# Where the second steps of a cross attention may place their divisions and layer-norm portions on VectorE

## The chip, the cores and the metric

The kernel runs on one core of one Trainium2 chip. The metric is the device time of one execution in microseconds (us). A core has a matrix engine (TensorE, PE in the profile, with its weight loads as PEld), a vector engine (VectorE, DVE), an activation engine (ScalarE, ACT), a general engine (GpSimd, POOL) and a queue that issues transfers (SyncE, SP). Each engine works through its own list of instructions in order, and waits on semaphores for the others.

## The reference, cut to what matters

The reference is one decoder layer in float32 over x of 16 batch elements, 112 tokens each, 512 features: self attention, cross attention over a context of 375 rows for each batch element, and a feed-forward part.

```python
q, k, v = heads(hs @ Wq.T + bq), heads(at @ Wk.T + bk), heads(at @ Wv.T + bv)   # 16 heads of 32
scores = clip(q k^T / sqrt(32), -50, 50); masked keys get -50
probs = softmax(scores)
ctx = probs @ v
delta = residual_scale * (ctx @ Wo.T + bo)
x = x + layernorm(delta) * ln_gamma + ln_beta
x = x + FFN(layernorm(x))        # after the cross attention
```

The change touches only the order of the cross attention's work. What is computed stays the same.

## The kernel before, in words

The kernel is written in a framework that traces instructions in the order of the program and then plans an issue order for each engine. TensorE is the exception: its order is that of the program. For the other engines the planner runs the program against a clock of its own, and whenever an engine is free it takes, of the instructions that are ready by that clock, the one that was traced first. So an instruction that was traced late can be issued early, if its inputs are there and the engine is free. `tc.issue_after(ins)` limits that: what the block traces on the engine of `ins` is queued behind `ins` in that engine's list. It adds no wait for another engine.

The cross attention runs over 16 batch elements b, and in each over three chunks kc of 125 keys. This text calls one turn of `cross.step` (line 1318) step (b, kc), and (b, 1) the second step of its batch element. A step lays, in this order:

- TensorE's 32 score matmuls of its keys (`scores`, line 929);
- ScalarE's two exponentials of them (line 1330), into tiles es for kc = 0 and e for the others;
- for the step before, called `late` in the code: TensorE's weighted values (`weigh`, line 940); VectorE's two additions of its e to es (`add`, line 1367), only if that step had kc = 1 or 2; and, if it had kc = 2, TensorE's key sums (line 951), ScalarE's copies of sums and values (lines 1376 and 1378), and a new generator `self.parts` with the divisions;
- ScalarE's check of the scores (line 1338);
- filler work for TensorE (`f.fill`), a queue of pieces that is worked off by estimated microseconds;
- portions of `self.parts`: two of them if kc = 1, the rest if kc = 2. A portion (`quotients`, line 1381) is a reciprocal (line 1383) and a multiplication (line 1384) on VectorE. Where b is a multiple of 4, all four are laid in the first step, with no tie.

The main loop then lays portions of `finish`, again only where kc > 0 and b is no multiple of 4: three portions for b = 1, 5, 9, 13, two for b = 2, 6, ..., three for b = 3, 7, .... In block 1 `finish` holds the second layer norm's rest (a reciprocal root of some 12 small instructions, lines 784 to 796, then one normalised row tile for each portion, line 802). In blocks 5 and 9 it holds the cross attention's own layer norm: a reciprocal root (with line 1287), then one row tile for each portion (lines 1291, 1299, 776 and 777), then the third layer norm's root and normalised tiles. It is used up in blocks 1, 6 and 10.

Both kinds of portions are laid under `issue_after(self.last)`, and `self.last` is the latest addition of line 1367. In step (b, 2) that is the addition of the step's own turn, for (b, 1). In step (b, 1) no addition is laid, so `self.last` is still that of step (b, 0), which belongs to the third chunk of batch element b - 1.

The filler of a block makes the keys and values of the next batch element. The first values are one product of eight matmuls (line 902), which VectorE copies out of its bank (line 907). The others come from seven block products for the values (line 1073, taken out by VectorE at lines 1076 and 1078) and seven for the keys (line 1013, taken out at lines 1035, 1023 and 1019), laid in turns; they are called r1 to r7 and k1 to k7 below. In odd blocks four products for queries follow (line 884, taken out by ScalarE at line 892). All these products, and the key sums, take turns in three PSUM banks with the tag mm: TensorE cannot begin a product before the bank of an earlier one has been emptied. VectorE also makes the sums of the context's blocks (line 979), and GpSimd one copy of keys (line 1203).

```python
            if b > 0 and kc > 0:
                with tc.issue_after(self.last):
                    for _ in range(2 if kc == 1 else C):
                        next(self.parts, None)
...
            if bl > 0 and kc > 0:
                with tc.issue_after(cross.last):
                    for _ in range(2 + bl % 2):
                        next(finish, None)
```

Of the kernel before, what the change touches and what calls it, by code (L numbers as in the profile page):

```python
# [597 lines left out]
def finite_layer(  # L598
# [30 lines left out]
    nc = tc.nc  # L629
# [22 lines left out]
    def pair(name, tag="e", bufs=3):  # L652
        return evp.tile([P, 2, HG, S], F32, tag=tag, name=name, bufs=bufs)
# [267 lines left out]
    def scores(k_of, q_of, rows_):  # L921

        scs = [psum("sc", [P, 2, 512]) for _ in range(2)]
        views = [
            s[:rows_, :, : HG * S].rearrange("p i (j s) -> p i j s", j=HG) for s in scs
        ]
        for j in range(C):
            for i in range(HG):
                nc.tensor.matmul(  # L929
                    views[i // 2][:, i % 2, j, :], k_of(i, j), q_of(i, j), start=True, stop=True  # L930
                )
        return views
# [179 lines left out]
    class SelfAttention:  # L1112
# [35 lines left out]
        def step(self, b, grp, f, us, prepared):  # L1148
            b, v, es = self.next
            if b + 1 < B:  # L1150
                self.begin(b + 1, grp)
            with tc.issue_after(self.behind.ins):
                for _ in range(prepared):
                    next(w2_prep, None)
            first = max(0.45 * us, min(us, 5.5))
            f.fill(first)
            eTs = []
            for e, share in zip(es, (0.45 * (us - first), 0.35 * (us - first))):
                tr = psum("sc", [P, 2, 512])
                trv = tr[:S, :, : HG * S].rearrange("p i (j s) -> p i j s", j=HG)  # L1160
                for i in range(2):
                    for j in range(C):
                        nc.tensor.transpose(trv[:, i, j, :], e[:, i, j, :], ident[:S, :S])  # L1163
                eT = pair("eT")
                nc.scalar.copy(eT[:S], trv)
                eTs.append(eT)
                f.fill(share)
            y = psum("ys", [P, C, S])
            weighted_values(y, v[b % GB][:S], eTs, True, True)
            nc.scalar.copy(xyT[:, :, ts(b, S)], y)  # L1170
            f.drain()
# [96 lines left out]
    class AfterCross:  # L1268
# [15 lines left out]
        def finish(self):  # L1284
# [23 lines left out]
                yield 0.0  # L1308
            yield from self.norm.steps()

    class Cross:


# [4 lines left out]
        def step(self, b, kc, q, keys, f, us):  # L1318
            scs = scores(
                lambda i, j: keys.third(keys.k[ds(i * DH, DH), j], kc),  # L1320
                lambda i, j: q[ds(i * DH, DH), j, ts(b % 2, S)],
                KP,
            )
            n = b * KC + kc
            late = self.late

            es = [(pair("es", "es", 3) if kc == 0 else pair("e"))[:KP] for _ in scs]
            self.late = (b, kc, keys.v[kc][:KP], es)
            for i, sc in enumerate(scs):
                nc.scalar.activation(  # L1330
                    es[i], sc, AF.Exp, scale=scl[:, n : n + 1], bias=bia[:, n : n + 1]
                )
            self.weigh(late)
            for i in range(2):
                self.add(late, i)
            self.divide(late)
            for i, sc in enumerate(scs):
                nc.scalar.activation(  # L1338
                    sc,
                    sc,  # L1340
                    AF.Relu,
                    scale=nscl[:, n : n + 1],
                    bias=limit[:KP, :1],
                    accum_out=low[:KP, 2 * n + i : 2 * n + i + 1],
                )
            if kc == 0 and b % GB == 0:
                for _ in self.parts:
                    pass
            f.fill(us)
# [4 lines that stand above are left out]
# [504 lines left out]
    def at_once(pieces):  # L1858
        run(pieces)
        yield from ()  # L1860

    def tiles_of(pieces):

        for _ in pieces:
            next(pieces, None)
            yield

    def tiles_of(pieces):
# [5 lines left out]
    late = itertools.chain(  # L1874
        itertools.repeat(None, 1),
        n3[2].transposes(),
        tiles_of(after[1].projections()),
        at_once(after[1].finish()),
        itertools.repeat(None, 3),
        n3[3].transposes(),  # L1880
    )
# [40 lines left out]
@with_exitstack  # L1922
def decoder_layer(ctx: ExitStack, tc: tile.TileContext, *args):
    nc = tc.nc
    flag = ctx.enter_context(tc.tile_pool(name="flag", bufs=1))
    unfit = flag.tile([1, 1], I32, name="unfit")
    finite_layer(tc, unfit, *args)
    with tc.If(nc.values_load(unfit, min_val=0, max_val=1, skip_runtime_bounds_check_because="a comparison gives 0 or 1") > 0):
        general_layer(tc, *args)
# [49 lines left out]
```

## Time and profile before

| what | value |
|---|---|
| median of 3 runs | 1358.8 us (1357.83 to 1360.26) |
| the profiled execution | 1359.02 us |
| its span, first to last instruction | 1357.2 us |
| TensorE busy | 1335.8 us of the span |
| VectorE busy | 819.8 us of the span |
| granted TensorE clock, mean | 0.998 |
| cross attention, 342 to 820 us: TensorE busy | 475.30 of 478.00 us |
| cross attention, 342 to 820 us: VectorE busy | 322.25 of 478.00 us |
| reciprocal, line 1383 | 64 times, mean 829 ns |
| multiplication, line 1384 | 64 times, median 263 ns |
| addition, line 1367 | 64 times, mean 1088 ns |

The time is 1.8 us more than the span; that lies around the first and the last instruction. All stretches below are microseconds from the start of the span. Steps are counted from the first score matmul of one to that of the next. Some of them: (1,0) is 364.57 to 376.06, (1,1) to 386.78, (1,2) to 396.27; (2,0) to 405.63; (5,0) is 491.48 to 504.68, (5,1) to 515.40, (5,2) to 525.45, (6,0) to 534.80; (9,0) is 623.65 to 635.14; (10,0) is 655.41 to 664.76; (12,0) is 714.66 to 725.26.

### The profile page before, as it was taken

The page shows a single profiled execution, that of the slowest core. Times are in us where ns is not written, and L with a number is a line of the kernel's source. Part 1 is how long each engine was busy: PE and PEld are TensorE (multiplying, and loading weights), DVE is VectorE, ACT ScalarE, POOL GpSimd, SP SyncE. Part 2 cuts the span into 40 slices and gives each one's busy share as a digit, 9 for nine tenths or more (in the row PEclk, how much of TensorE's full clock was granted, in tenths as well). Part 3 has the DMA queues.
Part 4 walks back from the last instruction along what each step waited for, and adds up shares of the span by engine and source line. Part 5 has one row for each costly group of instructions (what it writes and reads, how often), then busy time and mean ns, then how long its engine had stood idle before and what let it go on. Part 6 is the DMA issues. An engine that isn't in the chain of part 4 may idle for free.

```text
span 1357.2 us, 20739 instructions
## 1 busy us (share of the span) xinstructions
PE 1335.8 (98%) x8508; PEld 838.7 (62%) x8508; DVE 819.8 (60%) x1666; ACT 463.9 (34%) x909; POOL 47.5 (4%) x72
## 2 busy tenths in 40 slices
PE   8999999999999999999999999999999999999997
PEld 5555555556788778868887874544555555555553
DVE  3378987873656577657765578567653245554332
ACT  3345454553445535444546553101110011111000
POOL 3000010040000100000000000000000000000000
PEclk9999999999999999999999999999999999999999
DMA  9100002711111111111111111111131122321201
GB/s 313 62 1 32 1 16 79 259 40 24 27 28 28 36 28 28 29 26 28 44 38 28 32 48 31 47 47 47 39 117 62 47 62 70 93 83 72 93 0 57
DMA packets 93579, 76.16 MB, mean 56 GB/s; under 512 B 44657, under 2 KB 81568, under 8 KB 91172
## 3 DMA queue, kind: packets, MB, share of 16 engines
q1 hardware_dynamic: 91744, 71.51, 17.2%
q0 software_dynamic: 736, 1.65, 0.4%
q8 instruction: 69, 1.13, 0.4%
q10 hardware_dynamic: 996, 1.59, 0.3%
q14 instruction: 34, 0.28, 0.1%
HBM read 63.72 MB, written 11.01 MB: 55 GB/s over the span
## 4 chain that ended last, share of the span: by engine, by line
PE 92%; DVE 4%; ACT 1%; issue 1%; DMA 1%; POOL 0%; DVEq 0%; ACTq 0%; POOLq 0%
PE gate L1547 12%; PE mm L884 10%; PE mm L1013 9%; PE mm L902 8%; PE ys L1547 7%; PE mm L913 7%; PE mm L1073 6%; PE gate L1481 6%; PE mm L1547 5%; PE sc L929 5%; PE ys L940 4%; PE ys L1481 4%; PE mm L1481 3%; PE sc L1163 2%; PE mm L845 1%; PE mm L951 1%
## 5 line engine op out<-in xcount | busy, mean ns | idle before, releaser
L1330 ACT ACTIVATE e<-sc,bia,scl 125x896 f32<-125x896 f32 x64 | 68.5, 1095 | 133.9 <-PE sc L929 133.9
L1338 ACT ACTIVATE sc<-sc,limit,nscl 125x896 f32<-125x896 f32 x96 | 103.2, 1075 | 0.0
L1367 DVE TENSOR_TENSOR es<-es,e 125x896 f32<-125x896 f32 x64 | 68.9, 1088 | 55.7 <-ACT e L1330 55.6
L1547 PE MATMUL gate<-t,f 128*128 128x448 f32 x256 | 101.4, 539 | 0.0
L1481 PE MATMUL gate<-h,f 128*128 128x448 f32 x224 | 86.6, 539 | 0.0
L1130 ACT ACTIVATE e<-sc,mx 112x112 f32<-112x112 f32 x256 | 64.5, 402 | 51.4 <-DVE mx L1126 51.4
L1547 PE MATMUL gate<-xyT,f 128*128 128x448 f32 x192 | 80.1, 540 | 0.0
L1383 DVE RECIPROCAL r<-r 128x112 f32<-128x112 f32 x64 | 51.3, 829 | 45.3 <-ACT r L1376 45.3
L1547 PEld LDWEIGHTS gate<-t,f 128*128 128x128 f32 x256 | 48.6, 190 | 47.6 <-issue 47.2
L1547 PE MATMUL ys<-t,f 128*128 128x448 f32 x192 | 77.4, 539 | 0.0
L1563 ACT COPY u<-gate 128x448 f32<-128x448 f32 x16 | 8.5, 532 | 183.5 <-PE gate L1547 110.5
L1481 PEld LDWEIGHTS gate<-h,f 128*128 128x128 f32 x224 | 42.5, 190 | 41.3 <-issue 40.9
L902 PE MATMUL mm<-xv,cT 128*125 128x512 f32 x144 | 66.3, 602 | 0.0
L1013 PE MATMUL mm<-kt,xks 128*128 128x188 f32 x360 | 65.1, 324 | 0.0
L1013 PEld LDWEIGHTS mm<-kt,xks 128*128 128x128 f32 x360 | 59.7, 190 | 2.9 <-issue 0.7
L1547 PEld LDWEIGHTS ys<-t,f 128*128 128x128 f32 x192 | 36.5, 190 | 35.7 <-issue 35.5
L902 PE MATMUL mm<-wv,xyT 128*112 128x512 f32 x128 | 58.0, 596 | 0.0
L1125 DVE TENSOR_REDUCE mx<-sc 112x8 f32<-112x896 f32 x32 | 33.4, 1085 | 40.0 <-PE sc L929 40.0
L1493 DVE TENSOR_TENSOR h<-h,h 128x896 f32<-128x896 f32 x32 | 32.8, 1084 | 40.9 <-PE ys L1481 31.7
L1547 PEld LDWEIGHTS gate<-xyT,f 128*128 128x128 f32 x192 | 36.0, 190 | 34.4 <-issue 33.0
L929 PEld LDWEIGHTS sc<-q,kT 32*125 32x125 f32 x1536 | 46.2, 183 | 15.3 <-issue 14.5
L929 PE MATMUL sc<-q,kT 32*125 32x112 f32 x1536 | 54.7, 279 | 0.0
(221 smaller groups left out, 2415.3 us busy)
## 6 DMA issues: line engine op xcount, KB each, us to landing
f<-in_f_w SPq DMA_DIRECT2D x64, 256.0 KB, 3.2
f<-blocks SPq DMA_DIRECT2D x14, 1024.0 KB, 4.8
cT<-in_ctx SPq DMA_DIRECT2D x32, 250.0 KB, 3.8
w<-in_f_w SPq DMA_DIRECT2D x4, 1024.0 KB, 10.5
blocks<-w SPq DMA_DIRECT2D x4, 1024.0 KB, 5.5
cT<-in_ctx SPq DMA_DIRECT2D x32, 126.0 KB, 3.4
xr<-in_x SPq DMA_DIRECT2D x2, 1024.0 KB, 10.9
out_y<-o SPq DMA_DIRECT2D x8, 256.0 KB, 3.1
```

What stands on the lines that cost most here:

```text
L884: nc.tensor.matmul(acc[:, :n], w[:, c, ts(j, P)], src[:, c, :], start=(c == 0), stop=(c == C - 1))
L902: nc.tensor.matmul(acc[:n, :], src[:, c, :], w[:, c, :], start=(c == 0), stop=(c == C - 1))
L913: nc.tensor.matmul(acc, xyT[:, c, ts(t, P)], w[:, c, :], start=(c == 0), stop=(c == C - 1))
L929: nc.tensor.matmul(views[i // 2][:, i % 2, j, :], k_of(i, j), q_of(i, j), start=True, stop=True)
L1013: nc.tensor.matmul(acc[:, m], w[:, k, ts(m, P)], x[:, k], start=k == 0, stop=k == 1)
L1073: nc.tensor.matmul(acc, x[:, k, :n], w[:, k], start=k == 0, stop=k == 1)
L1130: nc.scalar.activation(e[:, i, j, :], sc[:, i, j, :], AF.Exp, scale=SCALE, bias=mx[:, i, j : j + 1],)
L1330: nc.scalar.activation(es[i], sc, AF.Exp, scale=scl[:, n : n + 1], bias=bia[:, n : n + 1])
L1338: nc.scalar.activation(sc, sc, AF.Relu, scale=nscl[:, n : n + 1], bias=limit[:KP, :1], accum_out=low[:KP, 2 * n + i : 2 * n + i + 1],)
L1367: self.last = nc.vector.tensor_tensor(total, total, late[3][i][:KP], ALU.add).ins
L1481: nc.tensor.matmul(banks[m][bank], o[:, c, ts(m, P)], t[:, c, :], start=first and c == 0, stop=c == UNITS - 1, skip_group_check=True,)
L1547: nc.tensor.matmul(bank, o[:, s, k, :], t[:, k, :], start=first and k == 0, stop=k == 1, skip_group_check=True,)
```

## The change

A function looks up the VectorE instruction that was traced last. In a second step, behind its scores, that instruction becomes `self.last`. So the portions of both kinds that are laid in step (b, 1) are queued behind the VectorE instruction that was traced last in step (b, 0), which is one that empties a product bank of that step's filler. In step (b, 2) the additions set `self.last` again, as before.

```diff
@@ -1308,6 +1308,14 @@
+    def latest():
+
+        return next(
+            i
+            for i in reversed(nc.cur_bb.bb.instructions)
+            if i.engine == mybir.EngineType.DVE
+        )
+
     class Cross:
@@ -1323,6 +1331,9 @@
             )
             n = b * KC + kc
             late = self.late
+            if late is not None and late[1] == 0:
+
+                self.last = latest()
 
             es = [(pair("es", "es", 3) if kc == 0 else pair("e"))[:KP] for _ in scs]
```

No instruction is added or removed, and none changes its operands.

## The prediction

> **What bounds the kernel now.** I read the page's first part, then TensorE's waits, then steps with equal matmul work side by side, then the order of VectorE around the steps that stood out.
>
> ```profile
> PE 1335.8 (98%) x8508; PEld 838.7 (62%) x8508; DVE 819.8 (60%) x1666; ACT 463.9 (34%) x909; POOL 47.5 (4%) x72
> ```
>
> TensorE is busy 98% of the span, and a change that only reorders VectorE can win no more than TensorE's idle time in the cross attention. There the front's table leaves 2.7 us of 478. The waits of TensorE from 400 to 820 us (total, times, longest):
>
> ```profile
> PE mm L1073 <- DVE v L907: 2.4, 2, 1.4
> PE mm L884 <- DVE kT L1023: 0.3, 1, 0.3
> ```
>
> So three waits make up nearly all of it: twice a value product waits for the copy of line 907 to empty a bank, once a query product waits for line 1023. Since matmul ends are modelled, I also compared steps with the same matmuls. The columns are length, then busy time of PE, PEld, DVE, ACT and POOL:
>
> ```profile
> 491.48:504.68 13.20, 11.76 (x110) 8.09 (x109) 12.08 (x37) 5.12 (x8) 0.66 (x1) 1.00 0.00 1
> 623.65:635.14 11.49, 11.49 (x109) 8.11 (x108) 9.63 (x23) 5.12 (x8) 0.40 (x1) 1.00 0.01 1
> 655.41:664.76 9.35, 9.35 (x97) 6.08 (x97) 5.94 (x14) 5.56 (x9) 0.00 (x0) 1.00 0.01 3
> 714.66:725.26 10.60, 9.62 (x97) 6.06 (x96) 5.23 (x12) 6.67 (x12) 0.00 (x0) 1.00 0.01 2
> ```
>
> Step (5,0) lasts 13.20 us, its equals (1,0), (9,0) and (13,0) each 11.49: 1.71 lost. Step (12,0) lasts 10.60, its equal (10,0) 9.35: 1.25 lost. Step (5,2) lasts 10.05, (9,2) 9.55: 0.50 lost. The whole prize is 3.5 us, 0.26% of the time. In (5,0) the loss comes about so:
>
> ```profile
> 496.63 1.41 DVE L1299 SCALAR_TENSOR_TENSOR xr<-d,rstd,xr 128x512 f32<-128x512 f32 x2
> 497.96 1.28 DVE L776 BATCH_NORM_STATS2 st<-xr 128x6 f32<-128x512 f32 x2
> 499.16 1.55 DVE L1383 RECIPROCAL r<-r 128x112 f32<-128x112 f32 x2
> 500.62 0.21 DVE L1384 TENSOR_TENSOR xyT<-xyT,r 128x112 f32<-128x112 f32 x1
> 500.75 0.68 DVE L907 COPY v<-mm 125x512 f32<-125x512 f32 x1
> ...
> 501.48 1.13 PE L1073 MATMUL mm<-xv,cT 128*125 128x256 f32 x4 [1.44 <-DVE v L907]
> ```
>
> The first value product ended at 497.91 (it began at 494.21 and took 3.70), but its copy was issued only at 500.75, behind portions that belong to step (5,1). They were early because their tie, the addition at 487.28, was already issued.
>
> **The change part by part.** No instruction appears or goes, no DMA, no wait on another engine. What moves are the portions of the second steps in the 12 blocks whose b is no multiple of 4. Their size: two reciprocals and two multiplications are 1.55 + 0.21 + 0.27 = 2.0 us in every block. In block 5 the root (lines 784 to 796 and 1287: 0.22 + 0.15 + 0.16 + 1.61 + 0.23 = 2.4), line 1291 twice (1.48), line 1299 (1.41), line 776 (1.28) and line 777 (0.24) add 6.8, together 8.8; block 9 has the same portions. Block 1 adds a root of 2.0 and two normalised tiles of 0.55 (together 5.1), blocks 6 and 10 two such tiles (3.1).
>
> *Step (5,0).* All 8.8 us leave it. The copy of line 907 can then start at 497.9, r2 need not wait, and the step should take 11.49: **1.71 won**. What is late next there is nothing, as (1,0) shows with quotients alone in front of the copy.
>
> *Step (12,0).* Its four portions are laid in the first step without a tie. The change does not reach them: 0.
>
> *Blocks 2 and 14, and 6 and 10.* The tie is the eviction of r2:
>
> ```profile
> 401.51 1.56 DVE L1383 RECIPROCAL r<-r 128x112 f32<-128x112 f32 x2 [5.09 <-ACT r L1376]
> 402.99 0.39 DVE L1384 TENSOR_TENSOR xyT<-xyT,r 128x112 f32<-128x112 f32 x2
> 403.30 0.68 DVE L907 COPY v<-mm 125x512 f32<-125x512 f32 x1
> ...
> 405.74 0.42 DVE L1078 TENSOR_TENSOR v<-mm,v 125x256 f32<-125x256 f32 x1
> ...
> 407.93 2.09 DVE L1367 TENSOR_TENSOR es<-es,e 125x896 f32<-125x896 f32 x2 [1.77 <-ACT e L1330]
> ```
>
> Leaving 401.51 wins nothing, since TensorE did not wait there. Behind 406.16 VectorE stood idle for 1.77 us until the exponential came; 2.0 us go in, the additions start 0.2 late. Behind them stands the eviction of k3 (it ended at 410.67), and r4 begins at 411.12: slack 0.45. So 0 in blocks 2 and 14, with 0.2 each as the upper end. In 6 and 10 it is 3.1 us into 1.78: 1.3 late. If the planner takes k3's eviction, which was traced earlier, ahead of the additions, nothing is lost; if not, 1.3 - 0.45 = 0.85. I take 0.1 each, nearer to the first, because the eviction has the older trace. Without the idle gap these 2.0 us would stand in front of evictions.
>
> *Blocks 3, 7 and 11.* The tie is the eviction of k3:
>
> ```profile
> 434.80 0.55 DVE L1019 TENSOR_TENSOR kT<-mm,kT 128x376 f32<-128x376 f32 x1 [1.40 <-PE mm L1013]
> 437.00 1.09 DVE L1367 TENSOR_TENSOR es<-es,e 125x896 f32<-125x896 f32 x1 [1.65 <-ACT e L1330]
> ```
>
> 2.0 us go into 1.65: 0.35 late. Here nothing is spare: r4's bank was emptied at 439.76 and k5 began at 439.81. Between 0 (if r3's eviction is taken ahead of the addition) and 0.35, I take 0.2 in each of three blocks: **0.6 lost**.
>
> *Blocks 1 and 13.* The tie is r3's eviction, issued at 379.37 behind the first addition of the step, because its values tile is free only after step (1,1)'s weighted values. From 378.36 to 387.66 VectorE has no gap, so the 2.33 us idle before cannot be used. The portions come between evictions, as those of the third step did (381.50, 382.99, 383.17), and push those back. Evictions were traced earlier and go first, so one is late by one reciprocal at most: 0.84, less a slack of 0.48. Lower end 0, upper 0.4 each; I take 0, since the old rows show the same mix without a wait.
>
> *Blocks 5 and 9.* Same tie, but 8.8 us into a stretch where VectorE is already busy 8.28 of 10.72 us and then 9.51 of 10.05. It runs on into (6,0), where it was idle for 4.56 us before 530.68. On the way lie the eviction of k7 (slack 0 in (5,2), where 0.50 was lost already) and the additions of (5,2), which the key sums need. Ends: -0.5 (that loss goes) and +4 each (rival B). I take 0.1 each, by the old (9,0), which carried the same portions with VectorE full from 615.18 to 628.58 and no wait.
>
> *Block 15.* Three projections instead of products; the banks have room: 0.
>
> A row on GpSimd: its copy of line 1203 took 0.40 us at 446.61 but 1.32 at 391.18, beside an addition at 391.15 that took its usual 1.09. The Trainium skill ("SBUF — State Buffer", section "Summary: rules for kernel authors") says that a VectorE instruction with two SBUF inputs and a GpSimd read block each other, the later one until the first is done. This speaks against a denser VectorE: by it, where the copy comes first, VectorE would lose up to 0.4 us in each of 12 blocks, an estimate of 4.8 us; by the row the loss falls on GpSimd, for which nobody waits, and it is 0. No row shows VectorE as the loser.
>
> Sum on the profiled execution: 1359.0 - 1.7 + 0.6 + 0.2 (blocks 6 and 10) + 0.2 (blocks 5 and 9) = 1358.3. That execution stood 0.2 above the median, so **1358.1** against 1358.8.
>
> **The rivals.** 0.2% is 2.7 us here, about what a measurement of this kernel can tell from no change; it puts the bounds at 1356.1 and 1361.5.
>
> A, the forecast: one stall goes, small ones come. Its own ends are 1356.6 (no new loss, and (5,2) cured too) and 1360.0. Chance 0.52.
>
> B, slower: the portions of blocks 5 and 9 get in front of the additions. The second addition of (5,2) ended at 523.17 and the key sums began at 527.31, so the margin is 4.1 us; in block 9 it is 653.20 and 657.27, again 4.1. VectorE is idle for about 0.4 us on the way. If all 8.8 are issued first, the key sums come 8.8 - 0.4 - 4.1 = 4.3 late, in two blocks 8.6: about 1366. For: the portions were traced before the additions. Against: a root is a chain, with gaps in which the old order let an addition in (519.53). It begins to cost from 4.5 us in front, and with 3.8 us lost in both it is over the bound. Chance 0.20, spread from 1361 to 1367.
>
> C, faster: the planner's clock shifts and (12,0) and (5,2) are cured as well: 1358.8 - 3.5 = 1355.3. Against it: (12,0) is not tied. Chance 0.08.
>
> D, the change does not do what it says: VectorE is still full when the first value product of (6,0) or (10,0) ends, and the wait for line 907 comes back there, 1.0 to 1.7 us once or twice: 1358.4 to 1360.5. For: VectorE was issuing 2.8 us late in the old (5,0) after 13 us without a gap. Chance 0.20.
>
> **How the numbers follow.** Faster: C and the lowest part of A, 0.10. Slower: B and a little of D, 0.23. The same: 0.67. The range goes from 1355.8 to 1362.5; it leaves out most of B and about half of C, some 0.17.
>
> **What would show it.** Right: (5,0) takes 11.5, (12,0) still 10.6, reciprocals stand between lines 1078 and 1367 in step (2,1), (3,1) grows from 10.86 by 0.1 to 0.35. Wrong: a wait of line 951 for line 1367, or of line 1073 for line 907 at 530 or 660 us, or a new one in (5,1) or (9,1).

## The result and the profile after

The changed kernel takes 1361.05 us (median of 17 runs, 1360.60 to 1363.63) against 1358.48 us for the kernel before in the same sessions (17 runs, 1357.71 to 1360.99). The ratio is 1.0019, 95% interval 1.0012 to 1.0027: 2.6 us lost where 0.7 us (1358.1 against 1358.8) had been forecast as won. The time lies inside the range that was given, on the other side of no change.

The busy times of the page of the changed kernel answer to those of before:

```profile
PE 1340.3 (98%) x8508; PEld 840.3 (62%) x8508; DVE 818.9 (60%) x1666; ACT 462.7 (34%) x909; POOL 49.2 (4%) x72
```

The same instructions, and VectorE is no busier. The profiled execution took 1363.63 us (span 1361.9), which is 2.6 above the median of its kernel. It is taken apart below, because not all of it is the change. TensorE's waits from 400 to 820 us in the changed kernel (total, times, longest; those of (1,2) and (15,2) lie outside and are shown further down):

```profile
PE mm L1073 <- DVE v L907: 1.0, 1, 1.0
PE mm L884 <- DVE kT L1023: 0.6, 1, 0.6
PE mm L1073 <- DVE kT L1023: 0.6, 2, 0.3
PE mm L951 <- DVE es L1378: 0.2, 1, 0.2
```

Lines behind the new function have moved in the listing: in the changed kernel the addition is line 1378, the division lines 1394 and 1395, the exponential line 1341, the check line 1397. One of the two waits for line 907 has gone, and there are two new kinds: a value product waits for line 1023, and the key sums wait for an addition. Steps (5,0), (10,0) and (12,0) of the changed kernel, with the columns of before (length, then busy time of PE, PEld, DVE, ACT, POOL):

```profile
493.81:505.30 11.49, 11.49 (x109) 8.11 (x108) 5.31 (x12) 5.11 (x8) 0.58 (x1) 1.00 0.00 0
657.00:667.49 10.49, 10.28 (x97) 6.21 (x96) 8.33 (x27) 5.56 (x9) 0.00 (x0) 1.00 0.01 2
717.98:728.58 10.60, 9.62 (x97) 6.07 (x96) 5.23 (x12) 6.67 (x12) 0.00 (x0) 1.00 0.01 2
```

Step (5,0) has the 11.49 us of its equals, (12,0) is unchanged at 10.60, and (10,0) has grown from 9.35 to 10.49. In (5,0) the copy of line 907 now starts as soon as its product has ended:

```profile
500.27 0.69 DVE L907 COPY v<-mm 125x512 f32<-125x512 f32 x1 [4.05 <-PE mm L902]
```

VectorE's busy time in (5,0) has fallen from 12.08 to 5.31, and in (10,0) it has grown from 5.94 to 8.33: part of the pushed work arrives there. The steps were then compared one by one, from the first score matmul of one to that of the next, (15,2) to the first gate matmul behind it. Steps not named differ by less than 0.04 us:

| step | before, us | change, us | blocks that share the cause |
|---|---|---|---|
| (5,0) | 13.20 | -1.70 | 5 |
| (5,2) | 10.05 | -0.47 | 5 |
| (1,2) | 9.50 | +0.77 | 1 |
| (3,1), (7,1), (11,1) | 10.86 | +0.04, +0.04, +0.05 | 3, 7, 11 |
| (6,1), (10,1) | 8.58 | +0.54, +0.54 | 6, 10 |
| (9,2) | 9.54 | +0.84 | 9 |
| (10,0) | 9.35 | +1.14 | 9 |
| (15,2) | 7.67 | +1.02 | 15 |
| sum | | +2.83 | |

The sum agrees with the 2.57 us between the medians. The span grew by more, 4.7 us: 1.52 us of the rest lie in front of the cross attention and 0.4 behind it. Those in front come from 17 to 22.5 us. The windows of before and of after there (the last three columns are granted clock, DMA share and GB/s):

```profile
17.00:22.50 5.50, 4.47 (x14) 2.43 (x15) 3.41 (x13) 1.70 (x3) 0.41 (x1) 1.00 1.06 389
```

```profile
17.00:22.50 5.50, 4.62 (x10) 2.39 (x11) 3.21 (x13) 1.03 (x2) 0.26 (x1) 0.69 1.06 388
```

The clock was granted at 0.69 in this execution, where it was 1.00 in that of before, and the 32 matmuls of line 884 that run then took 13.99 us instead of 12.29. The change does not reach that stretch, and other profiled executions fall on either side (last section). It is left out of all that follows: steps are compared by their own lengths.

**Where the time is lost.** There are four places. In (9,2) and (10,0), the order of VectorE and the waits of TensorE in the changed kernel:

```profile
651.05 0.74 DVE L1291 SCALAR_TENSOR_TENSOR d<-d,seen,gamma 128x512 f32<-128x512 f32 x1
...
651.79 1.08 DVE L1378 TENSOR_TENSOR es<-es,e 125x896 f32<-125x896 f32 x1
...
652.86 0.40 DVE L1023 SCALAR_TENSOR_TENSOR kT<-mm,dbk,kT 128x188 f32<-128x188 f32 x1
...
657.60 1.27 DVE L776 BATCH_NORM_STATS2 st<-xr 128x6 f32<-128x512 f32 x2
...
658.88 1.05 DVE L1378 TENSOR_TENSOR es<-es,e 125x896 f32<-125x896 f32 x1
```

```profile
653.77 3.29 PE L884 MATMUL mm<-xyT,xq 128*128 128x224 f32 x16 [0.62 <-DVE kT L1023]
...
659.99 0.94 PE L951 MATMUL mm<-es,ones 125*32 125x448 f32 x4 [0.21 <-DVE es L1378]
```

The eviction of the last key product (line 1023) comes at 652.86, behind two divisions, the root, line 1291 twice and the first addition, and a query product waits for its bank. Counted from the step's first score matmul, its first half starts 6.25 us in (652.86, the step at 646.61), where before it started 5.54 us in (651.40, the step at 645.86); its second half is now later still (653.31). The row of before:

```profile
651.40 0.73 DVE L1023 SCALAR_TENSOR_TENSOR kT<-mm,dbk,kT 128x188 f32<-128x188 f32 x2
```

The second addition comes at 658.88, behind four row tiles (lines 1299, 776, 777), and the key sums wait for it: 0.21 us by the matmuls' records, 1.01 by those of their weight loads. In (1,2) the same happens to line 1023 behind block 1's normalised tiles and an addition:

```profile
391.72 1.92 DVE L802 TENSOR_SCALAR xn<-xr,seen,rstd 128x512 f32<-128x512 f32 x4
393.56 1.08 DVE L1378 TENSOR_TENSOR es<-es,e 125x896 f32<-125x896 f32 x1
394.56 0.73 DVE L1023 SCALAR_TENSOR_TENSOR kT<-mm,dbk,kT 128x188 f32<-128x188 f32 x2
```

with the query product waiting 0.50 at 395.34. In (6,1), and with the same rows in (10,1), the portions push two additions behind them, and these stand in front of k3's eviction:

```profile
537.19 1.00 DVE L802 TENSOR_SCALAR xn<-xr,seen,rstd 128x512 f32<-128x512 f32 x2
538.10 2.09 DVE L1378 TENSOR_TENSOR es<-es,e 125x896 f32<-125x896 f32 x2
540.11 0.73 DVE L1023 SCALAR_TENSOR_TENSOR kT<-mm,dbk,kT 128x188 f32<-128x188 f32 x2
```

so that r4 waits 0.28 at 540.89. In (15,2) it is ScalarE that TensorE waits for. ScalarE's list of the changed kernel, then its check in the kernel before, then TensorE's wait in the changed kernel:

```profile
817.19 0.67 ACT L1397 ACTIVATE r<-r,limit 128x448 f32<-128x448 f32 x1 [3.01 <-DVE xyT L1395]
817.76 0.19 ACT L1397 ACTIVATION_READ_ACCUMULATOR r<-r,limit 128x1 f32 x1
817.85 1.08 ACT L1341 ACTIVATE e<-sc,bia,scl 125x896 f32<-125x896 f32 x1
```

```profile
812.84 0.67 ACT L1386 ACTIVATE r<-r,limit 128x448 f32<-128x448 f32 x1 [1.99 <-DVE xyT L1384]
```

```profile
821.05 0.86 PE L940 MATMUL ys<-e,v 125*32 125x112 f32 x26 [0.70 <-ACT e L1341]
```

The check of the quotients is the next instruction in ScalarE's list, and it waits 3.01 us for the last multiplication (816.90 on VectorE). The exponentials behind it need nothing from it and wait with it: the check starts 2.83 us into the step where before it started 1.80 in (812.84, the step at 811.04), which is the step's whole loss.

### The profile page after: what moved, and what is told of

It is laid out like the page before. It is cut to its first block, busy times and chain, and to the rows that moved or that the text cites. A ratio compares the mean times of both kernels' runs of the same rounds, so it can differ in the third digit from the quotient of the medians.

```text
span 1361.9 us, 20744 instructions
## 1 busy us (share of the span) xinstructions
PE 1340.3 (98%) x8508; PEld 840.3 (62%) x8508; DVE 818.9 (60%) x1666; ACT 462.7 (34%) x909; POOL 49.2 (4%) x72
## 4 chain that ended last, share of the span: by engine, by line
PE 91%; DVE 5%; ACT 2%; DMA 1%; issue 1%; POOL 0%; SPq 0%; ACTq 0%; DVEq 0%; POOLq 0%
PE gate L1558 12%; PE mm L884 10%; PE mm L1013 9%; PE mm L902 8%; PE ys L1558 7%; PE mm L1073 7%; PE gate L1492 6%; PE mm L913 6%; PE mm L1558 5%; PE sc L929 4%; PE ys L940 4%; PE ys L1492 4%; PE mm L1492 3%; PE sc L1163 2%; PE mm L845 1%; PE mm L951 1%
```

## The experiments

All of them write the change in another form, so that each kind of portion can be tied by itself and in chosen blocks. With both kinds tied and the condition b > 0 it is the changed kernel:

```diff
-            if late is not None and late[1] == 0:
-
-                self.last = latest()
+            self.tie = latest() if kc == 1 and b > 0 else None
...
-                with tc.issue_after(self.last):
+                with tc.issue_after(self.tie or self.last):
...
-                with tc.issue_after(cross.last):
+                with tc.issue_after(cross.tie or cross.last):
```

Times are medians, each beside runs of the kernel before on the same chip (1358.5 to 1358.7 us); steps are from the profiled execution, as changes against before.

**Only the divisions (q_only).** The second replacement above is left out for `finish`: only `self.tie or self.last` is used.

> Only the divisions of the second steps are tied to the VectorE instruction traced last; the finish portions stay tied to the additions. Theory (finish portions and block 15 make the loss): (5,0) loses its wait nearly whole, -1.5 to -1.7, because the copy of line 907 was 2.8 late and 2.0 of that go; (15,2) keeps +1.0; (1,2), (9,2), (10,0), (6,1) and (10,1) are as before the change. Cross attention -0.6 against the kernel before, time about 1358. Rival (the divisions themselves thicken the second steps): the losses of (1,2), (9,2), (10,0) and (10,1) stay, cross attention about +2 or more, time above 1360.

Measured: 1358.45 us, ratio 0.9997 (0.9988 to 1.0006). Steps: (5,0) -1.39, (5,2) +0.33, (9,2) +0.40, (3,1), (7,1), (11,1) +0.04 each, (15,2) +1.03, sum +0.51. (1,2), (6,1), (10,0) and (10,1) have not moved, as the theory said, but it had not expected the losses in (5,2) and (9,2), and its sum was -0.6.

**Only the finish portions (f_only).** The other way round: only `cross.tie or cross.last` is used.

> Only the finish portions of the second steps are tied to the VectorE instruction traced last; the divisions stay tied to the additions. Theory: (5,0) about -1.7 and (5,2) -0.5 as in the changed kernel; (1,2) +0.8, (9,2) +0.8, (10,0) +1.1 stay; (6,1) and (10,1) go to 0, since two tiles of 1.1 us alone fit the idle 1.8; (15,2) 0. Cross attention about +0.5, time about 1359. Rival (the divisions make the loss): only the gains stay, -2.2, time about 1356.3.

Measured: 1358.47 us, ratio 0.9997 (0.9988 to 1.0006). Steps: (5,0) -1.70, (5,2) +0.17, (9,2) +1.22, sum -0.31; all others 0. The theory missed here: (1,2) and (10,0) lose nothing with these portions alone, and (5,2) does not gain. Its rival missed too, because (9,2) loses. What follows from the two runs: the loss of (15,2) belongs to the divisions alone. The losses of (1,2) (0, 0, together +0.77), of (10,0) (0, 0, together +1.14) and of (6,1) and (10,1) (0, 0, together +0.54 each) are not sums: either kind alone fits into what room there is, both do not. (9,2) loses with 2.0 us of divisions 0.40, with 6.8 us of finish portions 1.22, and with both 0.84 there and 1.14 one step on. That fits a full list whose excess comes out at whatever is late last, but no run isolated it.

**Without block 15 (not15).**

```diff
-            self.tie = latest() if kc == 1 and b > 0 else None
+            self.tie = latest() if kc == 1 and 0 < b < B - 1 else None
```

> The change without its last block: in block 15 both kinds of portions are tied as in the kernel before. Theory (ScalarE's line 1386 check of the sums waits for the late multiplications and holds up the exponentials of (15,2) behind it): (15,2) goes back by 1.0, all other steps as in the changed kernel; cross attention +1.8, time about 1360.1. Rival (the end of the cross attention is late for another reason, such as the projections' additions): (15,2) stays at +1.0, time 1361.

Measured: 1360.43 us, ratio 1.0012 (1.0003 to 1.0021). (15,2) is back at 0, all other steps are those of the changed kernel, sum +1.83. The loss of (15,2) comes from the tie in block 15 and from nothing else.

**Block 5 alone (only5).**

```diff
-            self.tie = latest() if kc == 1 and b > 0 else None
+            self.tie = latest() if kc == 1 and b == 5 else None
```

> The change in block 5 alone. Theory: (5,0) -1.7, (5,2) -0.5, nothing else; cross attention -2.2, time about 1356.3, ratio 0.9984. Rival (block 5 escaped a loss only because blocks around it were moved as well, block 6's tiles out of (5,2) above all): (5,2) or (6,0) gains 0.5 to 2 us of waits for lines 1023 or 1367, cross attention -1.2 to +0.5.

Measured: 1357.8 us, ratio 0.9993 (0.9984 to 1.0002). Steps: (5,0) -1.70, (5,2) -0.46, but (6,0) +1.60, sum -0.54. The wait for line 907 has moved on by three steps. VectorE in this kernel (the division is lines 1392 and 1393 here):

```profile
529.16 1.46 DVE L802 TENSOR_SCALAR xn<-xr,seen,rstd 128x512 f32<-128x512 f32 x3
530.53 1.56 DVE L1392 RECIPROCAL r<-r 128x112 f32<-128x112 f32 x2
...
532.32 0.68 DVE L907 COPY v<-mm 125x512 f32<-125x512 f32 x1
```

Normalised tiles and divisions of block 6, free by their old tie, go in front of the copy, as in the old (5,0). The run's theory was wrong and its rival right. It is also rival D of the prediction, to its size (it had 1.0 to 1.7 us); in the changed kernel it does not come, because block 6 is tied too.

**Block 5, and the divisions of block 6 (five_q6).**

```diff
+            self.tie = latest() if kc == 1 and b in (5, 6) else None
...
+                with tc.issue_after((cross.tie if b == 5 else None) or cross.last):
```

> Tied to the VectorE instruction traced last: both kinds of portions in block 5, the divisions alone in block 6, nothing else. Block 5 alone had moved its wait on to (6,0), +1.6, where three tiles and block 6's two divisions stood in front of the copy of line 907. Theory (VectorE's list is full from (5,1) on, and whatever may still be issued early lands in front of that copy): with the divisions of block 6 held back, 1.9 us less stands there, (6,0) goes to 0 and (6,1) stays at 0, because 2.0 us fit the idle 1.8. (5,0) -1.7, (5,2) -0.5: cross attention -2.2, time about 1356.3. Rival (the list of block 5 itself is too full, block 6 is only where it shows): (6,0) keeps 1 us or more, cross attention about -1, time about 1357.5.

Measured: 1356.73 us, ratio 0.9985 (0.9976 to 0.9994). Steps: (5,0) -1.70, (5,2) -0.47, nothing else, sum -2.16, as the theory had it. So (6,0) is kept by the divisions alone, and (6,1) loses nothing with 2.0 us in front of its additions instead of 3.1.

**The same, and block 12's divisions in its later steps (five_q6_12).** Here the four portions of block 12, which before were all laid in its first step, are laid in its second and third as in other blocks.

```diff
-            if kc == 0 and b % GB == 0:
+            if kc == 0 and b % GB == 0 and b // GB < NG - 1:
                 for _ in self.parts:
                     pass
```

> As five_q6, and in block 12 the four divisions are no longer laid in the first step but in the second and third, as in blocks that are no multiple of 4 (nothing needs them before the last block). Theory (the wait of (12,0) is the same as that of (5,0): portions in front of the copy of line 907): (12,0) falls from 10.60 to 9.35, as (10,0), -1.25; cross attention -3.4, time about 1355.1, ratio 0.9975. Rival (the wait of (12,0) comes from somewhere else, or moves to (12,1)): (12,0) and (12,1) together lose less than 0.5.

Measured: 1355.75 us, ratio 0.9975 (0.9965 to 0.9986). (12,0) -1.25 besides, sum -3.41. The prize named in the prediction, 3.5 us, is real and nearly all of it can be had; no wait of TensorE is listed in the cross attention any more.

**A tie to the copy of line 907 (tie907).** The tie is not the last eviction of the first step but its first copy, in all blocks but those with b a multiple of 4 and 15.

```diff
+            self.tie = keys_copy[-1] if kc == 1 and b % GB > 0 and b < B - 1 else None
...
-                v[:KP], xv, self.third(self.c, kc), nc.vector.tensor_copy
+                v[:KP], xv, self.third(self.c, kc), lambda *a: keys_copy.append(nc.vector.tensor_copy(*a).ins)
```

> The portions of the second steps are tied to the copy of line 907 in the first step instead of the instruction traced last, in all blocks that are no multiple of 4 except 15. Theory (the loss grows with how much is pushed into the full second and third steps; only the copy needs protection): (5,0) -1.2 to -1.7; divisions are back in the first steps, so (6,1) and (10,1) are 0 to 0.3; (1,2), (9,2) and (10,0) lose less than in the changed kernel, together under 1.5 of its 2.75; cross attention -1.5 to +0.5, time 1357 to 1359. Rival (any hold of these portions costs the same, the tie's place does not matter): (1,2), (9,2), (10,0) lose 2.7 as in the changed kernel, cross attention about +1.5, time 1360.

Measured: 1361.8 us, ratio 1.0018 (1.0009 to 1.0027). Steps: (1,1) +0.14, (5,0) -1.70, (5,1) +1.32, (5,2) -0.12, (9,1) +1.33, (9,2) +1.03, all others 0, sum +1.99. The theory was wrong: an earlier place is no cheaper. The sum is near the changed kernel's without block 15 (+1.83), in other steps: now it is the evictions of line 1078 in (5,1) and (9,1) that are late, while (1,2), (6,1), (10,0) and (10,1) lose nothing. Blocks 5 and 9 have no place in front of the second step's evictions where 8.8 us cost nothing.

**The check traced later (check15, then check15b).** In the first try batch element 14's check was only traced at the end of the cross attention:

```diff
+            if b == B - 2:
+                self.held = b, r
+                return
...
+    cross.check(*cross.held)
     for _ in cross.parts:
```

> The changed kernel, with one ScalarE instruction moved: the check of the sums that block 15 lays for batch element 14 (line 1386) is laid behind the last matmuls of the cross attention. All ties and divisions stay. Theory (ScalarE's list is in order, and the check, waiting for late multiplications, holds the exponentials of (15,2)): (15,2) falls back by 1.0, cross attention +1.8, time about 1360.1. Rival (the divisions delay (15,2) on VectorE, for instance the additions or the projections' bank): (15,2) keeps about +1.0.

Measured: 1361.3 us, ratio 1.002 (1.0011 to 1.0029), all steps as in the changed kernel, (15,2) +1.02. This tells nothing: the planner, which takes what is ready by its clock, issued the check at the same place (815.64, after the same wait of 3.01 us). A later place in the program is no later place in the list. The second try ties it behind the last exponential of (15,2):

```diff
+                self.exp = nc.scalar.activation(es[i], sc, AF.Exp, ...).ins
...
+    with tc.issue_after(cross.exp):
+        cross.check(*cross.held)
```

> The whole change, with one ScalarE instruction moved: the check of batch element 14's quotients is queued behind step (15,2)'s last exponential instead of in front of its first. Theory (the check, made late by the moved divisions, keeps ScalarE from the exponentials in its order): (15,2) returns from +1.02 to 0 (at most +0.1), all other steps as in the changed kernel, steps together +1.8, time 1.0 us below the changed kernel's, about 1360.0. Rival (it is VectorE: the late multiplications keep the queries' and projections' banks, or the additions, in (15,2), and the check only shows it): (15,2) stays at +0.7 or more and the time at 1361.

Measured: 1360.0 us, ratio 1.001 (1.0001 to 1.002). (15,2) is at -0.41, less than the 0 to +0.1 of the theory, all other steps as in the changed kernel, sum +1.42. ScalarE of this kernel in the step (exponential 1339, check 1401):

```profile
814.00 1.10 ACT L1339 ACTIVATE e<-sc,bia,scl 125x896 f32<-125x896 f32 x1 [1.36 <-PE sc L929]
...
818.13 0.67 ACT L1401 ACTIVATE r<-r,limit 128x448 f32<-128x448 f32 x1
```

The divisions are as late as before and nothing is lost: the check alone carried the 1.02 us. The step is even 0.41 shorter than in the kernel before, where the check had already held back the exponentials (its wait of 1.99 us above). The last section shows where these 0.41 us had gone.

**Blocks 6 and 10 tied further back (late6).** The changed kernel, but there the tie is the VectorE instruction traced last at the end of the second step's filler, so that both additions and k3's eviction stand ahead of the portions.

```diff
             f.fill(us)
+            if kc == 1 and b in (6, 10):
+                self.tie = latest()
```

> The whole change, but in batch elements 6 and 10 the second step's portions are tied to the VectorE instruction traced last at the end of that step's filler instead of in front of it, so that both additions of (b,1) and k3's eviction stand ahead of the portions. Theory (3.1 us of portions made the additions late, and the pair of additions then stood in front of k3's eviction): (6,1) and (10,1) return from +0.54 each to 0, the portions fall into (6,2) and (10,2), where they cost 0 to 0.3 each; steps together +1.75 to +2.4, time 1360.0 to 1360.5. Rival (VectorE is simply full in these blocks, whatever the order, so the loss only moves): (6,2) and (10,2) lose 0.5 or more each, steps together +2.8 or more, time 1361 or more.

Measured: 1364.88 us, ratio 1.0045 (1.0028 to 1.0061). (6,1) and (10,1) are at 0 as the theory has it, but (6,2) and (10,2) lose 1.76 each, more than the theory allowed, and (15,2) 1.27, where the check now waits 3.25 us (why it waits longer than in the changed kernel is open); sum +5.53. The rival's time came true, and worse. In (6,2) its reason is not what the trace shows. ScalarE there, then VectorE, then TensorE:

```profile
544.15 0.67 ACT L1397 ACTIVATE r<-r,limit 128x448 f32<-128x448 f32 x1 [5.51 <-DVE xyT L1395]
...
544.81 1.08 ACT L1339 ACTIVATE e<-sc,bia,scl 125x896 f32<-125x896 f32 x1
```

```profile
545.92 1.09 DVE L1378 TENSOR_TENSOR es<-es,e 125x896 f32<-125x896 f32 x1 [0.90 <-ACT e L1339]
...
547.99 1.09 DVE L1378 TENSOR_TENSOR es<-es,e 125x896 f32<-125x896 f32 x1 [0.52 <-ACT e L1339]
549.00 0.75 DVE L1078 TENSOR_TENSOR v<-mm,v 125x256 f32<-125x256 f32 x2
```

```profile
549.81 1.54 PE L1013 MATMUL mm<-cT,xks 128*128 128x188 f32 x8 [1.15 <-DVE v L1078]
```

It is the mechanism of (15,2) with one link more: the check waits 5.51 us, the exponentials wait behind it, VectorE's additions wait for the exponentials, and behind the additions stands the eviction that TensorE needs.

**The same with every check behind the exponentials (late6_checks).**

```diff
-            nc.scalar.activation(
-                r, r, AF.Relu, scale=-1.0, bias=limit[:, 1:], accum_out=top[:, b : b + 1]
-            )
+            with tc.issue_after(self.exp):
+                nc.scalar.activation(
+                    r, r, AF.Relu, scale=-1.0, bias=limit[:, 1:], accum_out=top[:, b : b + 1]
+                )
```

> late6 with ScalarE's check of the quotients queued, in every block, behind the last exponential of the step in which the last division is laid. Found in late6: (6,1) and (10,1) went back to 0, but (6,2) and (10,2) lost 1.76 each. Theory (the portions cost nothing in themselves there; they made the last multiplication late, and the check, which waits 5.51 us for it at 544.15, stands in front of the exponentials at 544.81): (6,2) and (10,2) return to within 0.1 of the kernel before, (15,2) to 0 or a little below; (1,2) +0.77, (9,2) +0.84, (10,0) +1.14 stay; steps together +0.6 to +1.2, time about 1359.5. Rival (VectorE is full and the additions are late in themselves): (6,2) and (10,2) keep 0.5 or more each, steps together +1.8 or more, time 1360.5 or more.

Measured: 1359.96 us, ratio 1.0009 (0.9999 to 1.0018), sum +1.54. (6,2) falls from +1.76 to +0.16 and (15,2) to -0.41, but (10,2) only to +1.07. So the theory holds in block 6 and covers some 0.7 of 1.76 in block 10; the rest there is VectorE's own list, as the rival has it; that is read from the order, no further run tested it. Block 10 has four normalised tiles in that step (676.41, 1.91 us), block 6 two (544.03 in late6, 1.00), and behind them the additions and evictions are late:

```profile
676.41 1.91 DVE L802 TENSOR_SCALAR xn<-xr,seen,rstd 128x512 f32<-128x512 f32 x4
678.24 1.08 DVE L1378 TENSOR_TENSOR es<-es,e 125x896 f32<-125x896 f32 x1
```

**Only what won (best).** five_q6_12 with the checks of late6_checks.

> Only what won: in block 5 both kinds of portions tied as in the changed kernel, in block 6 the divisions alone, block 12's divisions laid in its second and third steps as in other blocks, and ScalarE's checks behind the exponentials as in the other kernel of this call. Theory: (5,0) -1.70, (5,2) -0.47, (12,0) -1.25 as in five_q6_12, and (15,2) -0.41 as in check15b; steps together -3.8, time 1355.4, ratio 0.9975 to 0.997. Rival (the checks, now behind the exponentials, hold back something else on ScalarE, the queries' copies of line 892 above all): steps (b,2) of odd blocks grow by 0.3 or more, steps together -3.0 or less of a gain, time 1356.2 or more.

Measured: 1354.6 us (1354.21 to 1354.85, 7 runs) against 1358.51, ratio 0.997 (0.9959 to 0.9981). Steps: (5,0) -1.70, (5,2) -0.47, (12,0) -1.25, (15,2) -0.41, all others 0, sum -3.81. It beats both kernels, the steps did what the theory said (the time is 0.8 us below its 1355.4), and each term of its sum came out as the earlier runs had it.

## Why the prediction was wrong

The forecast's sum had -0.7 us on the steps, measured are +2.83. Step by step:

| step of the prediction | said, us | measured, us | what the runs show |
|---|---|---|---|
| (5,0) | -1.71 | -1.70 | right, by the cause given |
| (12,0) | 0 | 0 | right |
| blocks 2 and 14 | 0 | 0 | right |
| blocks 3, 7, 11 | +0.2 each | +0.04 to +0.05 | right in kind, a quarter of the size: the divisions held the list for 1.78 us (437.56 to 439.34), not 2.0, and the addition came 0.05 late |
| block 13 | 0 | 0 | right |
| block 1 | 0 | +0.77 | wrong |
| blocks 6 and 10 | +0.1 each | +0.54 each | the other branch |
| block 5 | +0.1 | -0.47 | the lower end |
| block 9 | +0.1 | +1.98 | wrong: rival B's wait (1.14) and k7's eviction (0.84) |
| block 15 | 0 | +1.02 | wrong |

Steps that failed:

*"Block 15. Three projections instead of products; the banks have room: 0."* It looked only at who waits for VectorE's evictions. The two divisions that move are waited for by ScalarE's check, and behind the check stand the exponentials. not15 and check15b show it from both sides. The prediction never followed the moved instructions to their own reader, although the trace of before lists line 1386 as the one that waits for the multiplications (52.4 us in 16 waits).

*"Blocks 5 and 9 ... by the old (9,0)."* In the old (9,0) VectorE was full and nobody waited, but the root and two row tiles (the tiles from 623.84 to 628.15) had no addition behind them until step (9,1), so that row said nothing of the key sums. What moves is the same in both blocks, as said; what stands behind it is not. Block 9 has four row tiles and block 5 three (line 1291 occurs four times and three). In block 5 of the changed kernel the second addition still found a place in front of the first line 1299:

```profile
519.72 0.74 DVE L1291 SCALAR_TENSOR_TENSOR d<-d,seen,gamma 128x512 f32<-128x512 f32 x1
...
520.46 1.08 DVE L1378 TENSOR_TENSOR es<-es,e 125x896 f32<-125x896 f32 x1
...
522.37 1.08 DVE L1378 TENSOR_TENSOR es<-es,e 125x896 f32<-125x896 f32 x1
523.37 1.54 DVE L1299 SCALAR_TENSOR_TENSOR xr<-d,rstd,xr 128x512 f32<-128x512 f32 x2
```

The last small instructions of the root stand one by one in the list, with one other instruction between each two of them. In block 5 these places hold the third line 1291, the first addition, the two halves of line 1023 and the second addition. In block 9 the fourth line 1291 (651.05) has the place of the first addition, everything behind it moves on by one, and the second addition finds none: lines 1299, 776 and 777 stand in front of it for 5.2 us (653.64 to 658.88). This is read from the two lists; no run took the fourth row tile out. Rival B had this mechanism, with its margin of 4.1 us and a price from 4.5 us on, and the sign that was named for it, a wait of line 951 for line 1367 (1378 here), appeared. It came in one block only, at 1.14 us. The other 0.84 us are the eviction of k7, which the prediction had named too, with a slack of 0, and still took 0.1.

*"Blocks 1 and 13 ... I take 0."* Only the 2.0 us of divisions were placed. Block 1's own finish portions, which make it 5.1 us as the part-by-part list says, move too; the runs with one kind alone show 0 and 0, and only both together 0.77. In block 13, where `finish` is empty, the 0 held.

*"Blocks 6 and 10 ... nearer to the first, because the eviction has the older trace."* The branch was named and the wrong one taken. The additions stand ahead of k3's eviction in the list. Since the planner prefers the older trace, k3's product cannot have been done by its clock when the additions were taken; that is concluded from the order, the planner's clock was not read. In the trace the product ended at 538.47 (begun at 536.93, 1.54 long), after the first addition had started (538.10). 0.54 lies within the 0.85 that was given for this branch. With the portions behind the eviction (late6) these two steps are back at 0, and q_only and f_only show that either kind alone does no harm there.

That the time lies in the range is in part luck: its upper end left room for a part of rival B and for D, but of the 5.0 us that the steps lost only 1.14 came by B's mechanism and none by D's. The forecast's sign was wrong because two terms (blocks 1 and 9) were set to 0 or 0.1 on the strength of a row with less behind it, one (blocks 6 and 10) on the planner's preference for the older trace, and one (block 15) without asking who reads the moved result.

Of the rule that was weighed ("SBUF — State Buffer", section "Summary: rules for kernel authors", in the Trainium skill), the prediction said that no row shows VectorE as the loser. That was misread. Line 795 usually takes 0.16 us; in the kernel before it took 0.35 beside a copy of line 1203, and ended with the copy:

```profile
653.12 0.35 DVE L795 TENSOR_TENSOR rstd<-rstd 128x4 f32<-128x4 f32 x1
```

```profile
652.25 1.21 POOL L1203 COPY kT<-kT 128x252 f32<-128x252 f32 x1 [26.47 <-DMA cT<-in_ctx]
```

Eight VectorE instructions that began during such a copy took 0.08 to 0.20 us more than the median of their kind, 1.33 us together; in the changed kernel it was nine and 1.36 us. So either engine can lose, as the rule has it, but the change added next to nothing on VectorE, and the 4.8 us worked out from the rule did not come. GpSimd's copies took 719 ns in the mean before and 821 after, and nothing waits for them.

Not settled: why (9,2) loses more (1.22) with the finish portions alone than with both kinds (0.84). In the list of that run lines 1299 and 776 of two row tiles (from 648.35) stand in front of line 1023, which starts 6.71 us into the step (650.96, the step at 644.25) against 5.54 before; no run isolated it.

## What to carry to other kernels

Of an instruction that is moved back on its engine, follow its reader too: on an engine that works in order, one waiting reader holds up everything behind it, even what needs nothing from the moved work (here 1.02 us in one step and 1.60 of the 1.76 us in another, won back by moving the reader alone). Work pushed into full stretches is not additive: two kinds of portions that cost nothing each cost 0.5 to 1.1 us a step together, so count all that the stretch then holds, not the gap in front of it. The tie in all blocks lost 2.8 us on the steps. In block 5 alone, where the trace shows the stall, it won only 0.5, because the stall moved on to (6,0); with block 6's divisions held back as well it won 2.2. So a tie is worth laying where the trace shows a stall, and then the next copy of the same kind has to be looked at.

## What the runs showed that was not expected

Three of the profiled executions (the changed kernel, five_q6 and tie907) had their TensorE clock granted at 0.69 to 0.70 from 17 to 22.5 us, and began the cross attention 1.52, 1.74 and 1.74 us later than the kernel before. The ten other profiled executions of the experiments had it at 1.00 there and began the cross attention within 0.25 us of the kernel before. All have the same work in that stretch; what sets the clock there is open. A single profiled execution can so be off by more than half of the effect that is looked for. Comparing steps by their own lengths takes this out: the same edit gave the same change within 0.01 to 0.02 us from one profiled kernel to the next (-1.70 and -1.71 in (5,0), +0.77 and +0.78 in (1,2)).

A stall need not show among the waits of the matmuls. In (15,2) the check in front of the exponentials cost 0.41 us in the kernel before, and the list of the matmuls' waits has nothing for this step. The eight matmuls of the key sums only took longer, 1.34 us in the kernel before and 0.93 in check15b:

```profile
817.43 1.34 PE L951 MATMUL mm<-es,ones 125*32 125x448 f32 x8
```

```profile
819.22 0.93 PE L951 MATMUL mm<-es,ones 125*32 125x448 f32 x8
```

The waits of the weight loads in the kernel before do name it:

```profile
PEld mm L951 <- DVE es L1367: 0.3, 1, 0.3
```

The prediction went by the matmuls' waits and by steps that have an equal, and (15,2) has none, so its prize of 3.5 us was 0.4 short.
